# The attention's first key and value loads issued during the last prologue chunks instead of in one block

## The chip, the cores and the metric

The kernel runs on one core of one Trainium2 chip. The metric is the device time of one execution in microseconds; lower is better. The times of before are 1974.73, 1968.76 and 1974.77 us, median 1974.73 us. One further execution was profiled.

## What is computed

One transformer block over `x` (4096 rows of 512) with cross-attention to a context of 3202 rows, followed by a state-space recurrence. Cut to what matters here:

```
q, k, v = heads(norm(x), Wq), heads(norm(ctx), Wk), heads(norm(ctx), Wv)   # 8 heads of 64
attn    = softmax(q @ k.T / 8)
x       = x + (attn @ v) @ W_o.T + b_o
u       = (norm(x) @ W_in.T + b_in) @ Bmat
s       = silu(s @ A.T) + u_t          # a scan over the 4096 rows
out     = x + s @ Cmat + mod
```

The keys and values depend on the context alone, so they are made once, in a prologue, and written to two DRAM buffers; the attention reads them back piece by piece.

## The kernel before

**The prologue** is the loop `for c in range(NCH)` from line 607 on. It walks over 26 chunks of the context, 128 rows each; the last has 2 rows. For chunk c it loads chunk c + 5 (`load_chunk`, on SP's DMA queue), normalises chunk c + 3, forms the value product `pv` (L617), turns chunk c + 2 for the matmuls, copies `pv` to the tile `vs` on ACT (L630) and writes `vs` to the DRAM buffer `vd` (L631, SP's queue). After every fourth chunk, and after the last one, comes a group g of key products: for each of the four head pairs hp one product `pk` (L655), its copy with bias to a tile `ks` on ACT (L663) and the write of `ks` to the DRAM buffer `kd` (L668, SP's queue). Group 5 ends with chunk 23; group 6, the last, holds chunks 24 and 25, so its products are 130 keys wide.

The tiles `ks` come from a pool with three buffers. The fourth `ks` of group 6 therefore goes into the buffer of the first one, and ACT may write it only when the first one's DMA to `kd` has landed.

**The loads.** `load_k` (L366, its DMA is L372) and `load_v` (L375, L380) fetch one pair of chunks of the keys or values of one head pair, 128 KB, into the pool `kp`, which has 13 buffers for each, a whole head pair's worth. Before, at c = 25, ahead of the group of key products, the kernel issues 9 loads of keys and 5 of values for the first unit of the attention (`AHEAD_K - 1` and `AHEAD - 1`). In SP's queue they stand as one block of 14, behind the write of `vx` (L636) and ahead of the four `kd` writes of group 6.

**The attention** starts when the loop is done. Its order is set by a planner, the class `Plan`, whose pieces carry costs and due times; the pieces for the first unit are `sample` (L725, matmuls into `sm`), `scores` (L705, matmuls into `s`), `maximum` and `base` (reductions on DVE), `spread` (L747, PE), `weights` (L782, ACT, makes `p` from `s`), `product` (L839, PE, makes `po`) and the query product `pq_o` (L325). Each step of `scores` first issues the load of keys ten steps ahead and of values six steps ahead. In the built kernel the loads of key pieces 9 to 12 and value pieces 5 to 12 thus follow one by one, in between and behind the last `kd` writes.

The attention's PSUM tiles take the banks of the prologue's pools, which are closed before it starts. In the built order of before, the second `sample` matmul waits for ACT, which is reading the last `pk`.

Every DMA on a queue of this kernel waits, before it is issued, for the DMA eight places ahead of it; SP issues strictly in its order.

Of the kernel before, what the change touches and what calls it, by code (L numbers as in the profile page):

```python
# [23 lines left out]
NCH = 26  # L24
# [29 lines left out]
def keys(c):  # L54


    return CK if c < NCH - 1 else REST


def blocks(c):  # L60

    return 2 if c < NDC - 1 else 1


def key0(c):
    return c * CK
# [117 lines left out]
def xattn_ssm_kernel(  # L184
# [100 lines left out]
    def normalize(xt, n, name, later=False, pool=None):  # L285

        fs = factors(stats(xt, n, name, pool), n, name, pool)
        last = partial(scaled, xt, fs, n, name, pool)
        return last if later else last()
# [17 lines left out]
    def m_tile(shape, name):  # L307

        pool = m_pools.pop(0)
        m_pools.append(pool)  # L310
        return pool.tile(shape, F32, tag="m", name=name)
# [54 lines left out]
    def load_k(i, c):  # L366

        Q, hp, half = units[i]
        if half == 0 or Q == NQB - 1:
            t = kp.tile([P, 2 * CK], F32, tag="k", name=f"k_{Q}_{hp}_{half}_{c}")  # L370
            n = blocks(c) * CK
            nc.sync.dma_start(t[:, :n], kd[hp, c, :, :n])  # L372
            kts[Q, hp, c] = t

    def load_v(i, c):  # L375
        Q, hp, half = units[i]
        if half == 0 or Q == NQB - 1:
            t = kp.tile([CK, 2, P], F32, tag="v", name=f"v_{Q}_{hp}_{half}_{c}")
            n = blocks(c)
            nc.sync.dma_start(t[:, :n], vd[hp, c, :, :n])  # L380
            vts[Q, hp, c] = t
# [5 lines left out]
    steps = [(i, c) for i in range(len(units)) for c in range(NDC)]  # L387
    AHEAD_K, AHEAD, REF = 10, 6, 7
# [12 lines left out]
    def fetch_w(k, queue, part=slice(0, NC)):  # L401
        queue.dma_start(raw[k][:, part], wsrc[:, part, k * H : (k + 1) * H])

    def gain(k, w, i=None):
        for i in range(NC) if i is None else (i,):
            nc.vector.tensor_scalar(
                w[:, i, :], raw[k][:, i, :], g1s[:, i : i + 1], None, ALU.mult
            )

    def weighted(w, by, name):  # L410

        t = wp.tile([P, H], F32, tag="weighted", name=name, bufs=2)
        nc.vector.tensor_scalar(t, w[:, 0, :], by[:, 0:1], None, ALU.mult)
        for i in range(1, NC):
            nc.vector.scalar_tensor_tensor(t, w[:, i, :], by[:, i : i + 1], t, ALU.mult, ALU.add)
        return t

    def shift(k):

        t = weighted(raw[k], be1s, f"shift_{k}")  # L420
        yield
        pb = m_tile([P, 512], f"pb_{k}")
        for o in range(NC):
            nc.tensor.matmul(
                pb[:, o : o + 1], t[:, o * P : (o + 1) * P], ones[:, 0:1],
                start=True, stop=True,
            )
        yield
        nc.vector.tensor_tensor(
            bias[:, k * NC : (k + 1) * NC],  # L430
            pb[:, :NC],
            bqkv[:, k * NC : (k + 1) * NC],
            ALU.add,
        )
        yield
# [104 lines left out]
    def load_chunk(c):  # L540
        if c < NCH:
            n = keys(c)
            xt = cin.tile([CK, H], F32, tag="cx", name=f"cx_{c}", bufs=6)
            nc.sync.dma_start(xt[:n], ctx_in[key0(c) : key0(c) + n, :])
            cxs[c] = xt

    def norm_chunk(c):
        if c < NCH:
            xhs[c] = normalize(cxs.pop(c), keys(c), f"c{c}", pool=cin)
# [27 lines left out]
    with tc.manual_schedule():  # L577
        load_chunk(0)
        nc.scalar.dma_start(g1s, g1)
        fetch_w(2, nc.scalar, slice(0, NC // 2))  # L580
        fetch_w(2, nc.sync, slice(NC // 2, NC))
        load_chunk(1)
        load_chunk(2)
        fetch_w(1, nc.sync)
        load_chunk(3)
        idle = m_tile([P, 512], "idle")
        nc.scalar.copy(bu, neg_half)
        for _ in range(11):
            nc.tensor.matmul(idle[:, :P], a_t, a_t, start=True, stop=True)
        for t, src in ((be1s, beta1), (bqkv, b_qkv), (g2s, g2), (be2s, beta2)):  # L590
            nc.sync.dma_start(t, src)
        for c in range(4, 5):
            load_chunk(c)
        early = [first_chunk(c) for c in range(2)]
        next(early[0])
        next(early[0])
        turn_chunk(0)
        gain(2, wv, 0)
        gain(2, wv, 1)
        next(early[1])  # L600
        gain(2, wv, 2)
        norm_chunk(2)
        gain(2, wv, 3)
        next(early[1])
        work = side()
        first = shift(1)
        for c in range(NCH):
            load_chunk(c + 5)
            norm_chunk(c + 3)
            g, n = c // GC, keys(c)  # L610
            ct, o = cts[g], key0(c) - key0(g * GC)
            pv = kps.tile([P, 512], F32, tag="v", name=f"pv_{c}")
            parts = 1 if c < NCH - 1 else 2
            for i in range(NC // parts):
                for h in range(parts):
                    k = h * NC // parts + i
                    nc.tensor.matmul(  # L617
                        pv[h * HD : h * HD + n, :H],
                        ct[:, k, o : o + n],
                        wv[:, k, :],  # L620
                        start=(i == 0),
                        stop=(i == NC // parts - 1),
                        skip_group_check=True,
                    )
            if c == 0:
                turn_chunk(1)
            turn_chunk(c + 2)
            if c < NCH - 1:
                vs = cin.tile([CK, NC, P], F32, tag="vs", name=f"vs_{c}")
                nc.scalar.copy(vs, pv)  # L630
                nc.sync.dma_start(vd[:, c // 2, :, c % 2, :].rearrange("h p d -> p h d"), vs)  # L631
            else:
                second = wp.tile([n, H], F32, name="second")
                nc.scalar.copy(second, pv[HD : HD + n])
                nc.vector.tensor_tensor(vx[:n], pv[:n], second, ALU.add)
                nc.sync.dma_start(vx[HD : HD + n], vx[:n])  # L636
            if c < GC:
                if c == 1:
                    gain(1, wk)
                for _ in range((0, 0, 1, 2)[c]):  # L640
                    next(first)
            else:
                next(work, None)
            if c % GC < GC - 1 and c < NCH - 1:
                continue
            n_g = o + n
            if c == NCH - 1:
                for k in range(AHEAD_K - 1):
                    load_k(*steps[k])
                for k in range(AHEAD - 1):  # L650
                    load_v(*steps[k])
            for hp in range(NC):
                pk = kps.tile([P, 512], F32, tag="k", name=f"pk_{g}_{hp}")
                for i in range(NC):
                    nc.tensor.matmul(  # L655
                        pk[:, :n_g],
                        wk[:, i, hp * P : (hp + 1) * P],
                        ct[:, i, :n_g],
                        start=(i == 0),
                        stop=(i == NC - 1),  # L660
                    )
                ks = cin.tile([P, GC * CK], F32, tag="ks", name=f"ks_{g}_{hp}")
                nc.scalar.activation(  # L663
                    ks[:, :n_g], pk[:, :n_g], AF.Identity, bias=bias[:, NC + hp : NC + hp + 1]
                )
                for b in range(g * GC, c + 1, 2):
                    m, k = blocks(b // 2) * CK, key0(b) - key0(g * GC)
                    nc.sync.dma_start(kd[hp, b // 2, :, :m], ks[:, k : k + m])  # L668
                if g == 0:
                    nc.gpsimd.tensor_copy(kx[:, hp, REST:], ks[:, : HD - REST])  # L670
                elif c == NCH - 1:
                    nc.gpsimd.tensor_copy(kx[:, hp, :REST], ks[:, CK : CK + REST])
                for _ in range(2 if g > 1 else 1):
                    next(work, None)
        left = sum(1 for _ in work)
        assert left == 0, left
# [1316 lines left out]
```

## Time and profile before

| | |
|---|---|
| runs, us | 1974.73, 1968.76, 1974.77 |
| profiled execution, us | 1970.81 |
| its span in the trace, us | 1969.0 |
| granted TensorE clock, mean | 0.994 |
| PE busy, share of the span | 98% |
| DVE, ACT, POOL busy | 74%, 60%, 12% |

The profiled execution's own time is 1.8 us longer than the span that the trace covers. Times in the rows are microseconds from the start of the span. PE is the matmul engine and PEld its weight loads, DVE, ACT and POOL the other engines; SPq is SP's queue, on which the DMAs in question are issued. In a timeline a row gives the start, the time it takes (rows of the same kind are merged, with their number behind the x), the engine, the line, and in brackets the idle time before it and what ended that. A table of windows gives the busy time of each engine in a stretch, then the granted clock (1.00 is full speed), the share of time for which the DMA engines were busy, and the rate.

### The profile page before, as it was taken

The numbers are of one execution on the slowest core, as the hardware profiler recorded it, in microseconds if no ns is written. First come the engines' busy times: TensorE is split into PE (matmuls) and PEld (weight loads), VectorE is DVE, ScalarE is ACT, GpSimd is POOL, SyncE is SP. The second block draws the span as 40 slices with busy tenths as digits, with TensorE's granted clock in tenths as the row PEclk, the third lists the DMA queues.
The fourth block names the chain that finished last, engine by engine and source line by source line (L and its number), as shares of the span: only waits on it lengthen the run. The fifth ranks groups of instructions, "written<-read, shape, count | busy, mean of one in ns | idle before, by whom it ended". The sixth has DMA issues, their size and how long they took to land. (4 is left out here: it accounts for less than half of the span.)

```text
span 1969.0 us, 66936 instructions
## 1 busy us (share of the span) xinstructions
PE 1932.5 (98%) x29092; PEld 1260.9 (64%) x29092; DVE 1460.6 (74%) x1983; ACT 1172.2 (60%) x1632; POOL 227.3 (12%) x374
## 2 busy tenths in 40 slices
PE   9999899999999999999999999999999999999997
PEld 5444477666666666666667666666666676765674
DVE  4320289688877887788868887888788886877776
ACT  2233377566666666666656665666666675665653
POOL 2121000001200120002100120012001210011105
PEclk9999899999999999999999999999999999999999
DMA  6532323223432243232422342224322331544576
GB/s 195 171 104 62 100 80 99 71 80 89 125 85 83 74 113 82 70 100 78 111 61 88 91 125 79 80 85 115 88 76 78 103 91 45 152 129 133 153 192 218
DMA packets 246934, 204.28 MB, mean 104 GB/s; under 512 B 80808, under 2 KB 220072, under 8 KB 246636
## 3 DMA queue, kind: packets, MB, share of 16 engines
q1 hardware_dynamic: 242616, 193.32, 34.2%
q10 hardware_dynamic: 4020, 6.62, 1.2%
q8 instruction: 231, 3.78, 0.8%
q14 instruction: 67, 0.55, 0.1%
HBM read 156.32 MB, written 29.88 MB: 95 GB/s over the span
## 5 line engine op out<-in xcount | busy, mean ns | idle before, releaser
L782 ACT ACTIVATE p<-s,shifts 128x1024 f32<-128x1024 f32 (+1 forms) x832 | 891.0, 1082 | 482.7 <-PE s L705 474.3
L790 DVE TENSOR_TENSOR acc<-p,acc 128x1024 f32<-128x1024 f32 (+1 forms) x704 | 830.8, 1180 | 205.1 <-ACT p L782 171.3
L705 PE MATMUL s<-q,k 64*64 64x256 f32 x12800 | 836.8, 378 | 1.8 <-ACT p L782 1.8
L839 PE MATMUL po<-p,v 64*64 64x256 f32 x12800 | 835.4, 377 | 3.3 <-DVE o L888 2.9
L705 PEld LDWEIGHTS s<-q,k 64*64 64x64 f32 x12800 | 491.3, 133 | 215.2 <-issue 14.9
L839 PEld LDWEIGHTS po<-p,v 64*64 64x64 f32 x12800 | 485.4, 133 | 194.2 <-issue 13.0
L1109 POOL TENSOR_TENSOR xr<-xr,rowb 128x512 f32<-128x512 f32 x30 | 44.4, 1494 | 987.4 <-DMA xr<-in_x_dram 846.4
L911 DVE RECIPROCAL rd<-rd 128x256 f32<-128x256 f32 (+1 forms) x64 | 110.2, 1722 | 12.9 <-ACT rd L906 12.5
L325 PE MATMUL pq<-xn,wq 128*128 128x512 f32 x248 | 110.7, 598 | 0.0
L1115 PE MATMUL pa<-wo,o 128*128 128x512 f32 x240 | 107.0, 599 | 0.0
L617 PE MATMUL pv<-wv,ct 128*128 128x512 f32 (+1 forms) x208 | 92.6, 595 | 0.8 <-ACT ct L575 0.8
L655 PE MATMUL pk<-ct,wk 128*128 128x512 f32 (+1 forms) x224 | 88.9, 550 | 0.0
L575 DVE COPY ct<-tp_c 128x512 f32<-128x512 f32 (+1 forms) x13 | 8.4, 649 | 105.8 <-PE tp_c L296 105.8
L790 DVE TENSOR_TENSOR acc<-p,p 128x1024 f32<-128x1024 f32 x64 | 78.1, 1220 | 10.5 <-ACT p L782 10.5
L325 PEld LDWEIGHTS pq<-xn,wq 128*128 128x128 f32 x248 | 45.7, 190 | 55.5 <-issue 54.3
L1115 PEld LDWEIGHTS pa<-wo,o 128*128 128x128 f32 x240 | 44.4, 190 | 56.0 <-issue 55.3
L814 DVE TENSOR_TENSOR acc<-swap,acc 64x256 f32<-64x256 f32 x126 | 61.8, 490 | 11.1 <-ACT swap L809 9.4
L663 ACT ACTIVATE ks<-pk,bias 128x512 f32<-128x512 f32 (+1 forms) x28 | 18.0, 642 | 82.6 <-PE pk L655 66.7
L655 PEld LDWEIGHTS pk<-ct,wk 128*128 128x128 f32 x224 | 39.2, 190 | 42.6 <-issue 42.6
L617 PEld LDWEIGHTS pv<-wv,ct 128*128 128x128 f32 (+1 forms) x208 | 36.9, 186 | 43.2 <-issue 41.0
L809 ACT COPY swap<-acc 64x256 f32<-64x256 f32 x126 | 50.8, 404 | 17.4 <-DVE acc L797 14.9
L334 ACT ACTIVATE q<-pq,bias 128x512 f32<-128x512 f32 x31 | 21.3, 688 | 62.5 <-PE pq L325 62.5
(222 smaller groups left out, 1220.1 us busy)
## 6 DMA issues: line engine op xcount, KB each, us to landing
k<-kd SPq DMA_DIRECT2D x432, 128.0 KB, 2.3
v<-vd SPq DMA_DIRECT2D x432, 128.0 KB, 2.2
xn<-x SPq DMA_DIRECT2D x416, 32.0 KB, 1.9
xr<-in_x_dram SPq DMA_DIRECT2D x30, 256.0 KB, 3.7
x1d<-xr SPq DMA_DIRECT2D x30, 256.0 KB, 2.2
x<-in_x_dram SPq DMA_DIRECT2D x28, 256.0 KB, 3.3
cx<-in_ctx_dram SPq DMA_DIRECT2D x25, 256.0 KB, 3.9
vd<-vs SPq DMA_DIRECT2D x25, 256.0 KB, 2.4
```

The source lines that it names most:

```text
L325: nc.tensor.matmul(pq, wq[:, i, hp * P : (hp + 1) * P], xn[:, i, :], start=(i == 0), stop=(i == NC - 1),)
L617: nc.tensor.matmul(pv[h * HD : h * HD + n, :H], ct[:, k, o : o + n], wv[:, k, :], start=(i == 0), stop=(i == NC // parts - 1), skip_group_ ...
L655: nc.tensor.matmul(pk[:, :n_g], wk[:, i, hp * P : (hp + 1) * P], ct[:, i, :n_g], start=(i == 0), stop=(i == NC - 1),)
L705: nc.tensor.matmul(s[k0 : k0 + HD, a, b, :], kts[(*w["at"][:2], c)][r, b * CK + k0 : b * CK + k0 + HD], q[r], start=True, stop=True, skip_ ...
L782: nc.scalar.activation(t[:, :, :nb, :], w["ps"][c][:, :, :nb, :], AF.Exp, bias=w["shift"])
L790: nc.vector.tensor_tensor(w["acc"][:, :, :nb, :], t[:, :, :nb, :], before[:, :, :nb, :], ALU.add)
L809: nc.scalar.copy(w["swap"][r], of[(1 - k) * HD : (2 - k) * HD])
L814: nc.vector.tensor_tensor(of[r], w["swap"][r], of[r], ALU.add)
L839: nc.tensor.matmul(w["po"][a * HD : (a + 1) * HD, k, :QU], vts[Q, hp, c][r, b, a * HD : (a + 1) * HD], t[r, a, b, :], start=(c == 0 and b ...
L911: nc.vector.reciprocal(w["rd"][:, part], (w["pd"] if last else w["rd"])[:, part])
L1109: nc.gpsimd.tensor_tensor(v["x"], v["x"], rowb, ALU.add)
L1115: nc.tensor.matmul(v["pa"], o_t[Q, c, half][:, t * P : (t + 1) * P], wo[:, c, :], start=(c == 0), stop=(c == NC - 1),)
```

## The change

The block of 14 loads ahead of the last group of key products goes. Instead the loop takes them from a list, up to four in a chunk, from chunk 20 on, right after `load_chunk`:

```diff
         first = shift(1)
+        loads = [partial(load_k, *steps[k]) for k in range(AHEAD_K - 1)]
+        loads += [partial(load_v, *steps[k]) for k in range(AHEAD - 1)]
         for c in range(NCH):
             load_chunk(c + 5)
+            if c >= 2 * AHEAD_K:
+                for _ in range(4):
+                    if loads:
+                        loads.pop(0)()
             norm_chunk(c + 3)
...
             n_g = o + n
-            if c == NCH - 1:
-                for k in range(AHEAD_K - 1):
-                    load_k(*steps[k])
-                for k in range(AHEAD - 1):
-                    load_v(*steps[k])
             for hp in range(NC):
```

With 14 loads and four in a chunk, chunks 20 to 23 take 4, 4, 4 and 2. No load is added or left out. The instructions of PE, DVE, ACT and POOL keep their order; SP's DMAs alone change theirs. The order that is built puts some of the planner's own loads further ahead too. From chunk 20 on SP's queue is now (k0 is the load of key piece 0, v0 of value piece 0; `kd` 5.1 is the write of group 5, head pair 1):

```
before  cx 25 | vd 20 | vd 21 | vd 22 | vd 23 | kd 5.0 x2 | kd 5.1 x2 | kd 5.2 x2 | kd 5.3 x2
        vd 24 | vx | k0 to k8 | v0 to v4 | kd 6.0 | kd 6.1 | kd 6.2 | k9 | v5 | k10 | kd 6.3
        v6 | k11 | v7 | k12 | v8 to v12
after   cx 25 | k0 to k3 | vd 20 | k4 to k7 | vd 21 | k8 v0 v1 v2 k9 | vd 22 | v3 v4 v5 | vd 23
        kd 5.0 x2 | k10 v6 k11 | kd 5.1 x2 | v7 | kd 5.2 x2 | kd 5.3 x2 | vd 24 | vx
        kd 6.0 | kd 6.1 | kd 6.2 | k12 | kd 6.3 | v8 to v12
```

After, k10 waits for the first write of `kd` 5.0, k11 for the second and k12 for that of `kd` 6.0, since they read what these write.

## The prediction

> **What bounds the kernel now.** I read the page's shares first (PE is busy for 98% of the span), then windows of 20 us for a place where PE is not full, then the waits of that place, then the timelines of the queue and engines that the waits name. The stretch around the change, and everything behind it:
>
> ```profile
> 160.00:180.00 20.00, 20.00 (x57) 9.39 (x56) 1.36 (x3) 6.91 (x11) 0.00 (x0) 1.00 0.18 58
> 180.00:200.00 20.00, 20.00 (x54) 9.08 (x53) 0.26 (x2) 4.34 (x7) 1.03 (x3) 1.00 0.16 48
> 200.00:220.00 20.00, 16.53 (x67) 8.40 (x65) 0.68 (x1) 4.34 (x8) 0.56 (x3) 0.96 0.36 111
> 220.00:240.00 20.00, 15.27 (x190) 9.24 (x194) 8.16 (x13) 9.11 (x11) 0.19 (x1) 0.78 0.41 121
> ...
> 240.00:1940.00 1700.00, 1685.80 (x27976) 1133.98 (x27968) 1373.84 (x1777) 1089.29 (x1489) 177.85 (x253) 1.00 0.35 98
> ```
>
> Behind the bounds of a window stand its length and PE's busy time: 20.00 of 20 in the two up to 200 us, then 16.53 and 15.27, with the granted clock (the number after POOL's) down to 0.78. From 240 to 1940 us PE is busy for 1685.80 of 1700 us at full clock. So the kernel is bound by PE, and what PE gets back near 220 us moves all the rest forward. Who PE waits for there (waits between 200 and 240 us: total, times, longest):
>
> ```profile
> ACT ks L663 <- DMA kd<-ks: 8.8, 1, 8.8
> ...
> PE sm L725 <- ACT ks L663: 8.2, 1, 8.2
> ```
>
> One wait of 8.2 us. PE's sample matmul waits for ACT's `ks` of the fourth head pair, and that waits for a write to `kd`, the one whose buffer it reuses. SP's queue, ACT and PE over this time:
>
> ```profile
> 210.41 0.59 ACT L630 COPY vs<-pv 128x512 f32<-128x512 f32 x1 [2.70 <-PE pv L617]
> 211.02 0.37 SPq L631 DMA_DIRECT2D vd<-vs  x1
> 213.36 0.37 ACT L663 ACTIVATE ks<-pk,bias 128x130 f32<-128x130 f32 x1 [0.55 <-PE pk L655]
> 213.59 0.74 SPq L636 DMA_DIRECT2D vx<-vx  x1
> 214.38 4.18 SPq L372 DMA_DIRECT2D k<-kd  x9
> 215.89 0.64 PE L725 MATMUL sm<-q,kx 64*64 64x256 f32 x2
> 218.60 2.33 SPq L380 DMA_DIRECT2D v<-vd  x5
> 221.04 1.34 SPq L668 DMA_DIRECT2D kd<-ks  x3
> 224.31 0.37 ACT L663 ACTIVATE ks<-pk,bias 128x130 f32<-128x130 f32 x1 [8.78 <-DMA kd<-ks]
> 224.73 0.70 PE L725 MATMUL sm<-q,kx 64*64 64x256 f32 x3 [8.20 <-ACT ks L663]
> 225.23 3.58 PE L705 MATMUL s<-q,k 64*64 64x256 f32 x28
> 225.89 0.76 DVE L739 TENSOR_REDUCE m<-sm 128x1 f32<-128x256 f32 x2 [12.37 <-PE sm L725]
> 226.68 0.16 DVE L740 TENSOR_TENSOR m<-m 128x1 f32<-128x1 f32 x1
> 229.07 3.70 PE L325 MATMUL pq_o<-xn,wq 128*128 128x512 f32 x8
> 230.56 2.12 ACT L782 ACTIVATE p<-s,shifts 128x1024 f32<-128x1024 f32 x2
> ```
>
> The first `ks` of group 6 is ready at 213.36 + 0.37 = 213.73. SP is then busy with `vx` until 214.33 and with the 14 loads from 214.38 to 220.93, and starts that `ks`'s write at 221.04 only. PE ends its first sample matmuls at 215.89 + 0.64 = 216.53 and stands until 224.73. What the pause does to the clock:
>
> ```profile
> 218.00:218.50 0.50, 0.00 (x0) 0.00 (x0) 0.00 (x0) 0.00 (x0) 0.00 (x0) 0.91 0.90 283
> 218.50:219.00 0.50, 0.00 (x0) 0.00 (x0) 0.00 (x0) 0.00 (x0) 0.00 (x0) 0.50 0.78 221
> ...
> 228.00:228.50 0.50, 0.50 (x9) 0.26 (x7) 0.00 (x0) 0.00 (x0) 0.00 (x0) 0.50 0.56 162
> 228.50:229.00 0.50, 0.50 (x14) 0.30 (x6) 0.00 (x0) 0.00 (x0) 0.00 (x0) 0.85 0.75 194
> ...
> 224.73:228.62 3.89, 3.89 (x37) 2.28 (x40) 0.91 (x3) 0.00 (x0) 0.19 (x1) 0.50 0.62 178
> ```
>
> A mean of 0.91 over 218.00 to 218.50 is full clock until about 218.4 and half after it: the drop comes 1.9 us after PE went idle. The clock is whole again near 228.6, so PE's first 3.89 us after the pause run at half speed.
>
> **What is removed.** The 14 issues, (220.93 - 214.38) / 14 = 0.47 us each, no longer stand between `vx` and the write of `ks` 6.0. That write takes the place of the first load, at 214.38. How long it takes to land is known from its kind:
>
> ```profile
> DMA to landing us min/median/max: 1.7/1.7/1.8
> ...
> DMA to landing us min/median/max: 2.9/2.9/2.9
> ...
> DMA to landing us min/median/max: 1.7/1.8/3.7
> ...
> DMA to landing us min/median/max: 1.8/6.0/6.2
> ```
>
> These are the `kd` writes between 195 and 216 us, the very write of 221.04 behind 14 loads in flight, those between 100 and 125 us, and those between 35 and 45 us. 221.04 + 2.9 = 223.94, and ACT starts at 224.31: 0.37 from landing to ACT. Then 0.37 for ACT itself and 0.05 to PE. With 1.7, as the queue ahead of it holds only `vd` 24 (issued at 211.02) and `vx`: 214.38 + 1.7 + 0.37 + 0.37 + 0.05 = 216.87 for PE's restart. It saves 224.73 - 216.87 = **7.86 us** and leaves a pause of 0.34 us. The bounds: no pause at all gives 8.20; the slow landing of 2.9 gives 218.07, thus 6.66 with a pause of 1.54 us.
>
> **What goes with it.** Both pauses are shorter than the 1.9 us after which the clock fell, so I take the clock to stay. The 3.89 us at 0.50 then take half: **1.95 us** saved. That holds if PE, not DVE, sets the pace there: DVE began 225.89 - 224.73 = 1.16 us after the restart, at full clock half of that, 0.6, and L739 and L740 take 0.95 (to 226.84), thus 1.55 us after the restart. The score matmuls start 0.25 after it and take 3.58 / 2 = 1.8, until 2.05. The spread matmuls behind them find the maximum ready.
>
> The Trainium skill, "TensorE: Matmul & The Clock Gate", Part 1: The HAM clock gate, lets the clock fall after an idle window of about 3.4 us, in windows that run on their own. Here it fell after 1.9 us of idle, so the measurement decides, and the sum is the same by either, as 0.34 us is under both; the two part in the first rival.
>
> **What is added.** Nothing; 14 loads move ahead, and with them k9, k10, k11, v5, v6 and v7, which the built order pulls into chunks 22 to 23 and group 5. At 0.47 us each, at most five stand together (k8, v0, v1, v2, k9): 2.3 us of SP. SP has that time:
>
> ```profile
> SPq L631 <- ACT vs L630: 25.0, 5, 7.8
> SPq L668 <- ACT ks L663: 14.3, 5, 3.6
> ...
> 169.01 0.33 SPq L544 DMA_DIRECT2D cx<-in_ctx_dram  x1
> 172.33 21.39 SPq L631 DMA_DIRECT2D vd<-vs  x4
> 197.39 11.14 SPq L668 DMA_DIRECT2D kd<-ks  x8
> ...
> 192.75 0.59 ACT L630 COPY vs<-pv 128x512 f32<-128x512 f32 x1 [5.25 <-issue]
> 200.11 0.69 ACT L663 ACTIVATE ks<-pk,bias 128x512 f32<-128x512 f32 x1 [2.75 <-PE pk L655]
> ```
>
> Between 165 and 213 us it waits 25.0 us for `vs` copies and 14.3 us for `ks`, up to 7.8 us at a time. The first four loads fit behind the last `cx` load (169.34 to 171.2) ahead of `vd` 20 at 172.33. Without that cover a `vd` write would be 2.3 us late; its buffer is wanted again three chunks on (the copy of 192.75 reuses the one written at 172.33), so nobody would wait. PE, ACT and DVE have no instruction behind SP there. The transfers find the DMA engines at 0.18 and 0.16, in the first windows above; I cost all this at nothing.
>
> New are waits on SP: k10 and k11 for the writes of `kd` 5.0, with `kd` 5.1 behind them. With a landing of 1.7 us k10 is issued at 197.39 + 1.7 = 199.1, then v6 and k11 until about 200.5; the second `ks` of the group is done at 200.11 + 0.69 = 200.8. It hides. k12 waits for `kd` 6.0 (landed at 216.1), ahead of `kd` 6.3, whose `ks` is done at 216.82. `kd` 6.3 is issued near 216.9 and lands before 219.8 even with 2.9 us; the first `p`, which takes that room in SBUF, is due at 230.56 - 9.8 = 220.8. v8 to v12 keep their distance to `kd` 6.3.
>
> **Sum.** 7.86 + 1.95 = 9.8 us; the bounds give 6.66 + 1.95 = 8.6 and 8.20 + 1.95 = 10.15. Against the profiled execution's own 1970.81 us (span 1969.0 and 1.8 around it): 1961.0. The median of the runs, 1974.73, is 3.9 above it and one run 2.1 below; among these four executions the middle is (1970.81 + 1974.73) / 2 = 1972.8. From there the forecast is **1963.0 us**. Its own range is 1968.76 - 10.15 = 1958.6 to 1974.77 - 8.6 = 1966.2. A measurement here tells no change from one of about 0.3%, 5.9 us.
>
> **Rivals.** *The write lands late and the clock falls once more.* With 3.7 us, the longest `kd` landing once the weights are in (above), PE restarts at 218.87 after 2.34 us, past the 1.9 us: 5.86 us are won and nothing from the clock, 1972.8 - 5.9 = 1966.9, on the border of 0.3%. For it: 3.7 occurred. Against: at 214.38 no load is in flight. By the page's window of 3.4 us the clock would hold and the gain be 7.8.
>
> *The wait isn't removed*, because something other than the loads holds it: 1972.8. The write's start 0.11 us after the last load speaks against it. If a landing of 6.2 us recurred, the restart would be at 221.37 and the gain 3.4 us, 1969.4, also within 0.3%.
>
> *Slower: SP is blocked by its own reads.* If `kd` writes land after L us, k10 holds SP until 197.39 + L, `kd` 5.1's second half is issued 1.8 us later and lands at 199.2 + 2L; the first `ks` of group 6, which takes its buffer at 213.36, delays PE from L = 6.9 us on. The gain is used up at L = 11.8, and 0.3% is lost at L = 14.8 (9.8 + 5.9 = 15.7 us more in 2L): 1978.7 us. The longest L seen is 6.2, among the first weights; around 200 us it is 1.8.
>
> **How the numbers follow.** Forecast 80%, late landing with the clock 10%, wait not removed or half of it 6%, slower 4%. Faster by over 0.3%: nearly all of the first and half of the second, 0.83; within it 0.13; slower 0.04. The forecast's range, opened to 1957.5 for a lower run and to 1968.5 for most of the first rival, is the range.
>
> **What would show it.** In the profile of the changed kernel: `kd` 6.0 issued right behind `vx` near 214.4; PE's wait before the sample matmuls under 1.6 us, where it was 8.2; granted clock 1.00 throughout 200 to 240 us; the first `p` near 220.8; no wait of ACT or PE between 170 and 213 us that was not there before; the stretch behind unchanged but earlier. I am wrong if PE's busy time drops in the windows from 160 to 200 us, if the pause stays over 1.9 us, or if a wait of `p` or `po` for a DMA takes up what was won.

## The result

The changed kernel takes 1960.49 us (median of 6 runs, 1959.07 to 1964.69), the kernel before in the same series 1972.45 us (6 runs, 1968.76 to 1974.77). The ratio is 0.9944, 95% interval 0.9929 to 0.996: 11.0 us faster (7.9 to 14.0). The profiled executions are 1970.81 and 1960.71 us, 10.1 us apart.

The windows around the start of the attention, in the profile after (columns as before: length, busy time of PE, PEld, DVE, ACT and POOL, granted clock, DMA share, GB/s):

```profile
160.00:180.00 20.00, 20.00 (x57) 9.38 (x56) 1.45 (x3) 6.86 (x11) 0.00 (x0) 1.00 0.37 112
180.00:200.00 20.00, 20.00 (x54) 9.13 (x53) 0.17 (x1) 4.33 (x7) 1.02 (x3) 1.00 0.34 99
200.00:220.00 20.00, 19.74 (x114) 10.57 (x114) 2.11 (x7) 4.83 (x10) 0.74 (x4) 1.00 0.38 120
220.00:240.00 20.00, 20.00 (x327) 13.24 (x329) 14.21 (x13) 15.03 (x16) 0.00 (x0) 1.00 0.03 9
```

PE now lacks 0.26 us of the 40 from 200 to 240, where it lacked 8.20 before, and the clock is 1.00 in all of them. The loads show as DMA share 0.37 and 0.34 where it was 0.18 and 0.16; PE stays at 20.00 of 20 there. PE's wait for `ks` (waits of 200 to 240 us: total, times, longest):

```profile
PE sm L726 <- ACT ks L664: 0.3, 1, 0.3
```

And the timeline of SP's queue, ACT and PE over the last key products:

```profile
212.02 3.84 PE L656 MATMUL pk<-ct,wk 128*128 128x130 f32 x32
213.27 0.37 ACT L664 ACTIVATE ks<-pk,bias 128x130 f32<-128x130 f32 x1 [0.55 <-PE pk L656]
213.49 0.74 SPq L642 DMA_DIRECT2D vx<-vx  x1
214.35 1.57 SPq L669 DMA_DIRECT2D kd<-ks  x3
216.04 0.35 SPq L372 DMA_DIRECT2D k<-kd  x1
216.27 0.37 ACT L664 ACTIVATE ks<-pk,bias 128x130 f32<-128x130 f32 x1 [0.84 <-PE pk L656]
216.66 0.32 SPq L669 DMA_DIRECT2D kd<-ks  x1
216.69 0.44 PE L726 MATMUL sm<-q,kx 64*64 64x256 f32 x3 [0.26 <-ACT ks L664]
219.12 3.70 PE L325 MATMUL pq_o<-xn,wq 128*128 128x512 f32 x8
220.60 2.12 ACT L783 ACTIVATE p<-s,shifts 128x1024 f32<-128x1024 f32 x2
224.53 1.04 PE L840 MATMUL po<-p,v 64*64 64x256 f32 x16
```

The write of `ks` 6.0 follows `vx` at 214.35 instead of 221.04; ACT's fourth `ks` starts at 216.27 instead of 224.31, PE's sample matmuls at 216.69 instead of 224.73, the first `p` at 220.60 instead of 230.56.

For all comparisons below I take one distance within each trace, from the start of the last group's first `pk` to the start of the first `po`: it holds the whole disputed place, and what varies elsewhere between executions drops out. In the profile before its two ends are

```profile
212.12 3.84 PE L655 MATMUL pk<-ct,wk 128*128 128x130 f32 x32
...
234.48 1.04 PE L839 MATMUL po<-p,v 64*64 64x256 f32 x16
```

that is 22.36 us before and 224.53 - 212.02 = 12.51 us after: **9.85 us**. The 10.1 us between the profiled executions are this place almost alone.

### The profile page after: what moved, and what is told of

Its sections match the earlier page's. It is cut to its first block, busy times and chain, and to the rows that moved or that the text cites. A ratio compares the mean times of both kernels' runs of the same rounds, so it can differ in the third digit from the quotient of the medians.

```text
span 1958.9 us, 66935 instructions
## 1 busy us (share of the span) xinstructions
PE 1928.9 (98%) x29092; PEld 1259.3 (64%) x29092; DVE 1459.3 (74%) x1983; ACT 1171.3 (60%) x1632; POOL 225.5 (12%) x374
```

## The experiments

Two theories stood against mine, which was that the time came from the place of the write `kd` 6.0 in SP's queue and from the clock: that the early landing of the keys and values is what helps, and that the transfers in flight held the write. Each kernel of this table was timed beside the kernel before. The distances are worked out as above from the start of `pk` and of the first `po` in each trace. Each gain in the last column lies inside what the interval of its ratio allows.

| kernel | us, median | kernel before | ratio, 95% interval | `pk` to `po`, us | gain in it |
|---|---|---|---|---|---|
| changed | 1960.49 | 1972.45 | 0.9944 (0.9929 to 0.996) | 12.51 | 9.85 |
| block behind the products | 1968.08 | 1974.1 | 0.9961 (0.9947 to 0.9975) | 16.35 | 6.01 |
| own buffer for the fourth `ks` | 1968.66 | 1974.1 | 0.9968 (0.9958 to 0.9979) | 18.04 | 4.32 |
| filler on PE | 1970.86 | 1974.1 | 0.9985 (0.9975 to 0.9996) | 20.59 | 1.77 |
| `kd` writes from ACT's queue | 1962.92 | 1974.1 | 0.9944 (0.993 to 0.9957) | 12.39 | 9.97 |
| 4 loads left | 1964.15 | 1972.5 | 0.9957 (0.9943 to 0.9971) | 14.69 | 7.67 |
| 8 loads left | 1968.46 | 1972.5 | 0.9981 (0.9971 to 0.9991) | 18.71 | 3.65 |
| all 14 in chunk 20 | 1962.55 | 1972.5 | 0.9948 (0.9933 to 0.9962) | 12.51 | 9.85 |

**The block behind the last key products.** The kernel before with

```diff
-            if c == NCH - 1:
-                for k in range(AHEAD_K - 1): load_k(*steps[k])
-                for k in range(AHEAD - 1): load_v(*steps[k])
             for hp in range(NC):
...
+        for k in range(AHEAD_K - 1): load_k(*steps[k])
+        for k in range(AHEAD - 1): load_v(*steps[k])
         left = sum(1 for _ in work)
```

> The block of 14 loads is issued behind the last key products, so that SP's queue has vx, kd 6.0 to 6.3, then k0 to k8, v0 to v4. My theory (the time came from the place of kd 6.0 in SP's queue): kd 6.0 is issued near 214.4 and ACT's fourth ks starts near 216.4 as in the changed kernel, but k0 is now issued only near 217.0 and lands near 219.2 (2.2 us), so PE stands some 2.3 us before the first score matmul, and the first p comes near 223 if the clock holds, 224 to 225 if it falls: 5.5 to 7.5 us faster than before, 2.5 to 4.5 us slower than the changed kernel. Rival (the gain came from the early landing of the keys and values, the place of kd 6.0 does not matter): no gain, 1972 us.

Its timeline:

```profile
216.23 0.37 ACT L658 ACTIVATE ks<-pk,bias 128x130 f32<-128x130 f32 x1 [0.83 <-PE pk L650]
217.00 4.35 SPq L372 DMA_DIRECT2D k<-kd  x9
219.29 2.44 PE L704 MATMUL s<-q,k 64*64 64x256 f32 x32 [1.98 <-DMA k<-kd]
223.35 2.12 ACT L781 ACTIVATE p<-s,shifts 128x1024 f32<-128x1024 f32 x2
```

ACT's `ks` comes as early as in the changed kernel, though no load has moved ahead: the place of `kd` 6.0 alone does that. Then PE stands 1.98 us for k0, and the clock falls afterwards (at 220.6, for 3.4 us). It is 6.0 us faster than before, inside 5.5 to 7.5, and the rival that knows only the early landing falls. The rest of the changed kernel's gain is lost here because the loads now come later than before: k0 is issued at 217.00 instead of 214.38, and 12.51 becomes 16.35. Whether landing earlier than before is worth anything, this kernel can't say; the writes from ACT's queue below can.

**A buffer of its own for the fourth `ks`.** The block stays where it was:

```diff
-                ks = cin.tile([P, GC * CK], F32, tag="ks", name=f"ks_{g}_{hp}")
+                if c == NCH - 1 and hp == NC - 1:
+                    ks = cin.tile([P, CK + REST], F32, tag="ksl", name="ks_last", bufs=1)
+                else:
+                    ks = cin.tile([P, GC * CK], F32, tag="ks", name=f"ks_{g}_{hp}")
```

> The kernel before, but the fourth ks of the last group has a buffer of its own and waits for no write to kd. The block of loads stays ahead of the kd writes. My theory: PE's wait of 8.2 us before the sample matmuls goes wholly, the query product ends near 222.7, but the kd writes are still issued from 221.0 to 222.9 and land near 225.5, and the first p, which takes room that they read from, waits for them: the first p near 225 to 226 instead of 230.6 (before) and 220.6 (changed kernel), PE pauses some 2 to 4 us behind the query product, 4.5 to 5.5 us faster than before. Rival (the reuse of the ks buffer is the whole story): first p near 220.6, 10 us faster, as the changed kernel.

```profile
219.02 3.70 PE L325 MATMUL pq_o<-xn,wq 128*128 128x512 f32 x8
222.49 1.28 SPq L671 DMA_DIRECT2D kd<-ks  x3
223.89 0.35 SPq L671 DMA_DIRECT2D kd<-ks_last  x1
225.86 2.12 ACT L785 ACTIVATE p<-s,shifts 128x1024 f32<-128x1024 f32 x2 [5.23 <-DMA kd<-ks_last]
227.03 3.54 PE L708 MATMUL s<-q,k 64*64 64x256 f32 x32 [4.31 <-ACT p L785]
```

The wait of the prediction is gone, and the next one in line takes its place: the first `p`, in room that the `kd` writes read from, waits for the last of them, and PE stands 4.31 us behind the query product. So the buffer is the first thing that is held up, but not the cause; the cause is that the four writes stand behind the block. The first `p` came as expected; the gain of 4.32 us is a little under the 4.5 to 5.5. The writes began at 222.49 instead of 221.0, 0.9 us of it a wait of SP for an earlier load of `k` to land, and PE's pause was longer than the 2 to 4 us expected. The clock then fell at 227.24, so that `po` starts 3.30 us after the score matmuls of 227.03, where the changed kernel takes 1.78.

**PE kept busy.** The kernel before with work for PE in its pause, whose result nobody uses:

```diff
+        fill = m_tile([P, 512], "fill")
+        for _ in range(9):
+            nc.tensor.matmul(fill, wk[:, 0, :P], wk[:, 1, :], start=True, stop=True)
         left = sum(1 for _ in work)
```

> The kernel before, with nine 128x512 matmuls behind the last key products, whose result nobody uses; they fill 7.7 us of PE's pause. My theory (the half-speed stretch after the pause is due to PE's standing still): granted clock 1.00 throughout, restart of the sample matmuls still at 224.7, the query product begins 1.95 us earlier than the 229.07 of before, 1.9 us faster than before (1970.5 against 1972.45). Rival (the stretch is slow because the loads are in flight, or because a new kind of matmul begins): no gain, clock 0.50 after 224.7 or score matmuls as slow as before.

```profile
216.08 7.89 PE L677 MATMUL fill<-wk 128*128 128x512 f32 x18
225.16 0.44 PE L728 MATMUL sm<-q,kx 64*64 64x256 f32 x3 [0.61 <-ACT ks L663]
227.58 3.70 PE L325 MATMUL pq_o<-xn,wq 128*128 128x512 f32 x8
...
224.00:228.00 4.00, 3.38 (x49) 2.16 (x50) 1.22 (x5) 0.37 (x1) 0.18 (x1) 1.00 0.69 190
```

The restart is as late as before (12.76 us behind the start of `pk`, 12.61 before), but from it to the query product PE takes 227.58 - 225.16 = 2.42 us, as in the changed kernel (219.12 - 216.69 = 2.43), where the kernel before took 229.07 - 224.73 = 4.34. The clock is 1.00 with the loads in flight as before (DMA share 0.69). The half-speed stretch is thus the pause's, and its price here is 1.91 us.

**The `kd` writes of the last group from ACT's queue**, while SP issues the block:

```diff
-                    nc.sync.dma_start(kd[hp, b // 2, :, :m], ks[:, k : k + m])
+                    queue = nc.scalar if c == NCH - 1 else nc.sync
+                    queue.dma_start(kd[hp, b // 2, :, :m], ks[:, k : k + m])
```

> The kernel before, with the four kd writes of the last group issued from ACT's queue, right behind the ks that they write, while SP issues its block of 14 loads. My theory (place in SP's queue): kd 6.0 is issued near 213.9 and lands within 1.7 to 2.9 us, PE restarts between 216.6 and 217.6, clock 1.00: 8.8 to 10 us faster than before, within 1 us of the changed kernel. Rival (the transfers in flight delay the write, whoever issues it): kd 6.0 lands only when the block has, near 221 to 223, less than 3 us faster.

```profile
213.60 0.35 ACTq L669 DMA_DIRECT2D kd<-ks  x1
214.21 4.45 SPq L372 DMA_DIRECT2D k<-kd  x9
216.09 0.37 ACT L663 ACTIVATE ks<-pk,bias 128x130 f32<-128x130 f32 x1 [0.78 <-PE pk L655]
220.42 2.12 ACT L783 ACTIVATE p<-s,shifts 128x1024 f32<-128x1024 f32 x2
```

PE has no wait at all there, and the gain is the changed kernel's (9.97 against 9.85; the ratios are equal), with the block where it always was. `kd` 6.0 is ahead of the first load by 0.6 us in this kernel, so it doesn't show what a write in the midst of the block costs; the fourth write does, issued at 216.5: it took 3.4 us to land, and nobody waited for it. The block stands at its old time here and the gain is whole. So landing the loads earlier than before is worth nothing here; what costs is landing them later, as with the block behind.

**Some loads left behind.** The changed kernel, with n = 4 or 8 loads still between `vx` and the writes:

```diff
                 for _ in range(4):
-                    if loads:
+                    if len(loads) > n:
                         loads.pop(0)()
...
+            if c == NCH - 1:
+                for load in loads:
+                    load()
             for hp in range(NC):
```

> The changed kernel, but the last 4 of the 14 loads (v1 to v4) stay between vx and the kd writes; only 10 move ahead. My theory: kd 6.0 is issued 4 x 0.47 = 1.9 us later, near 216.3, lands after 1.7 to 2.5 us, and PE pauses 2.2 to 3.0 us. If the clock falls after about 1.9 us of pause, as in the kernel before, the score matmuls run at half speed for a while and the kernel is 3.5 to 5 us slower than the changed one; if it needs a whole idle window of 3.4 us, 1.9 to 2.7 us slower.

> The changed kernel, but 8 of the 14 loads (k6 to k8, v0 to v4) stay between vx and the kd writes. My theory: kd 6.0 is issued 8 x 0.47 = 3.8 us later, near 218.2, PE pauses 4.1 to 5.3 us, the clock falls: 5.7 to 7 us slower than the changed kernel, 3 to 4 us faster than before. The pause grows by 0.47 us with each load left. Rival (the wait goes with the block as a whole, for example with the transfers in flight): the pause does not grow with the number.

With 4 loads left, and below with 8:

```profile
216.42 1.32 SPq L672 DMA_DIRECT2D kd<-ks  x3
219.11 0.44 PE L729 MATMUL sm<-q,kx 64*64 64x256 f32 x3 [2.45 <-ACT ks L667]
...
218.00:219.00 1.00, 0.00 (x0) 0.00 (x0) 0.00 (x0) 0.32 (x1) 0.00 (x0) 1.00 0.44 100
219.00:220.00 1.00, 0.89 (x16) 0.67 (x20) 0.20 (x1) 0.05 (x1) 0.18 (x1) 1.00 0.89 261
```

```profile
217.94 1.39 SPq L672 DMA_DIRECT2D kd<-ks  x3
221.09 0.69 PE L729 MATMUL sm<-q,kx 64*64 64x256 f32 x3 [4.80 <-ACT ks L667]
...
221.00:222.00 1.00, 0.92 (x9) 0.56 (x13) 0.00 (x0) 0.03 (x1) 0.18 (x1) 0.54 0.78 232
224.00:225.00 1.00, 1.00 (x19) 0.57 (x14) 0.00 (x0) 0.00 (x0) 0.00 (x0) 0.75 0.71 203
```

The pause is 0.26, 2.45, 4.80 and 8.20 us for 0, 4, 8 and 14 loads: it grows by 0.57 us with each, more than the 0.47 us of its issue. The rest is landing: `kd` 6.0 took 1.5, 1.9, 2.3 and 2.9 us from its issue in these four traces, 0.1 us for each load ahead of it (in further executions 2.1 and 1.9 with 4 loads, 3.0 and 2.7 with 14). If that is the transfers' doing, which no run shows apart from the number of loads, their rival is right in a small part, 1.4 of the 7.94 us that ACT's fourth `ks` came sooner. With 8 the clock falls, and the distance is 6.20 us longer than the changed kernel's, inside 5.7 to 7. With 4, after 2.45 us of standing, the clock stayed at 1.00, and the distance is 2.18 us longer, as expected for that case.

**The clock once more.** That last row went against the reading of 1.9 us in the prediction, so the same kernel was profiled twice more, and the kernel before as well.

> The kernel of e4_leave_4 once more, for its clock. In e4_leave_4 PE paused 2.45 us and the clock stayed at 1.00, while in the kernel before it fell 1.9 us after the pause began. Theory: the clock is decided at the ends of windows of 3.4 us that run on their own (half-speed stretches so far: 10.3, 3.4, 3.4 and 3.4 us), and falls if more than about half of a window was idle; a pause of 2.45 us then falls into one window or is cut by an end, by chance, and in about 7 of 10 executions the clock falls for 3.4 us and costs up to 1.7 us. Rival: a pause of 2.45 us is too short for the clock; it stays at 1.00 again.

> As e7_leave_4_b, a third execution: by the theory of windows the pause of about 2.45 us makes the clock fall in some executions and not in others, always for a multiple of 3.4 us; by the rival it stays at 1.00 each time.

> The kernel before in another execution, for its clock. By the theory of windows of 3.4 us the pause of 8.2 us always makes the clock fall, but how long the matmuls run at half speed after it depends on where the next window ends: between 3.4 us and some 6 us, which costs 1.7 to 3 us; the first profile had 3.9 us (1.95). The wait of 8.2 us itself stays, within 0.3 us. Rival: the half-speed stretch is 3.9 us each time.

> As e8_before_b, a third execution: by the theory of windows a stretch between 3.4 and some 6 us that differs from the other two, by the rival 3.9 us again.

The kernel with 4 loads left, second and third execution:

```profile
219.30 0.69 PE L729 MATMUL sm<-q,kx 64*64 64x256 f32 x3 [2.71 <-ACT ks L667]
...
218.00:219.00 1.00, 0.00 (x0) 0.00 (x0) 0.00 (x0) 0.13 (x1) 0.00 (x0) 0.67 0.60 130
225.00:226.00 1.00, 1.00 (x4) 0.52 (x3) 0.00 (x0) 1.00 (x3) 0.00 (x0) 0.92 0.27 76
```

```profile
219.05 0.48 PE L729 MATMUL sm<-q,kx 64*64 64x256 f32 x3 [2.52 <-ACT ks L667]
...
219.00:220.00 1.00, 0.95 (x12) 0.73 (x16) 0.01 (x1) 0.00 (x0) 0.18 (x1) 0.66 0.97 263
222.00:223.00 1.00, 1.00 (x19) 0.61 (x14) 0.00 (x0) 0.00 (x0) 0.00 (x0) 0.64 0.67 189
```

and the third execution of the kernel before:

```profile
224.90 0.70 PE L725 MATMUL sm<-q,kx 64*64 64x256 f32 x3 [8.01 <-ACT ks L663]
...
220.00:221.00 1.00, 0.00 (x0) 0.00 (x0) 0.00 (x0) 0.00 (x0) 0.00 (x0) 0.76 0.92 289
230.00:231.00 1.00, 1.00 (x2) 0.35 (x2) 0.20 (x2) 0.67 (x2) 0.00 (x0) 0.62 0.52 139
```

Pauses of the same length (2.45, 2.71, 2.52 us) left the clock whole once and brought it down twice, in the last only after PE had restarted. A mean of 0.67 over 218 to 219 places the fall at 218.34, one of 0.92 over 225 to 226 the rise at 225.16: 6.8 us; in the third 219.32 and 222.72: 3.4 us. The second execution of the kernel before was like the first (22.38 us from `pk` to `po`); in the third the fall came at 220.52 and the rise at 230.76, so that 5.86 us behind the restart ran at half speed and the distance was 23.09 us. From the restart to the end of the query product these two took 4.26 + 3.70 and 4.67 + 4.27 us, the changed kernel 2.43 + 3.70: the clock's share in the kernel before is thus 1.8 to 2.8 us by execution, not a fixed 1.95. Both rivals fall, that a pause of 2.45 us always leaves the clock whole and that the half-speed stretch is 3.9 us each time; what the theory says is weighed at the end.

**All 14 loads in chunk 20**: the changed kernel with `for _ in range(14)` in place of `range(4)`.

> The changed kernel, but all 14 loads are issued in chunk 20 at once. My theory: SP has the time there (it waits for vs copies), vd 20 is issued near 175.9 instead of 172.2 and nobody waits for it; first p near 220.6 and the same time as the changed kernel, within 0.5 us in the trace. Rival (the spreading itself matters, a block of 14 delays what is behind it wherever it stands): a wait of PE or ACT of 1 us or more between 172 and 200 us, slower than the changed kernel by that.

```profile
212.07 3.84 PE L656 MATMUL pk<-ct,wk 128*128 128x130 f32 x32
...
224.58 1.04 PE L840 MATMUL po<-p,v 64*64 64x256 f32 x16
```

The distance is 12.51 us, the changed kernel's to the hundredth. `vd` 20 goes out at 175.96, there is no wait of PE between 100 and 240 us but the 0.3 us for `ks`, and ACT's waits between 170 and 213 us are the changed kernel's. That the loads are spread over chunks adds nothing; what counts is that they leave the place ahead of the `kd` writes.

## Why the prediction was right

**What bounds.** Right: PE's one long pause, 8.20 us, is now 0.26, and the windows behind are as full as before, only earlier.

**The write's new place.** `kd` 6.0 was put at 214.38 and came at 214.35. I took 1.7 us for its landing, as for the larger writes before it; it took 1.5. The row of 216.27 puts ACT's wait down to `pk`, but in the kernel with a buffer of its own, where the copy waits for no write, it starts 3.88 us after the start of `pk` and here 4.25: the landing still ends this wait, and the 0.26 us of PE are what is left of it. The restart, forecast at 216.87, was at 216.69; 0.10 of that is a prologue that ran so much earlier in this execution (212.02 against 212.12). The term of 7.86 us measured 224.31 - 212.12 less 216.27 - 212.02, 7.94: 6.59 from the issue and 1.4 from the landing. The prediction had both in one term and put 1.2 us of it (2.9 - 1.7) down to the landing; the series of loads left parts them.

**The clock.** The term of 1.95 us measured 4.34 - 2.43 = 1.91, and the filler shows it by itself. Sum 9.85 against the forecast 9.81.

**What was costed at nothing** was nothing: PE is full in the windows from 160 to 200 us, and ACT's waits between 170 and 213 us are those of before within 0.1 us. Of the reads that now wait on SP for their own writes, k10 was forecast at 199.1 and the second pair of writes to be on time (`ks` 5.1 done at 200.70):

```profile
199.05 0.32 SPq L372 DMA_DIRECT2D k<-kd  x1
199.94 0.38 SPq L372 DMA_DIRECT2D k<-kd  x1
200.73 0.79 SPq L669 DMA_DIRECT2D kd<-ks  x2
```

k11 is done at 200.32 and the pair goes out at 200.73: a slack of 0.4 us on SP, so this cover is thin. Behind it `kd` 6.3 was issued at 216.66 (forecast 216.9), in time for `p`; the own-buffer kernel shows what that wait costs when it isn't.

**Where a step was wrong.** "Both pauses are shorter than the 1.9 us after which the clock fell" took one distance in one execution for a limit. The conclusion held, 0.26 us being far from it; the first rival did not. It had the clock fall at a pause of 2.34 us, and the runs show that at 2.5 us it falls or not by the execution, sometimes only after PE has restarted; in one execution 1.76 us of standing had been enough when it fell. Nor did the write land late: 1.5 us.

**The time.** Forecast 1963.0, measured 1960.49, by the ratio 11.0 us (7.9 to 14.0) where the sum was 9.8. The interval holds the sum. One of the three profiles of the kernel before took 0.7 us longer over the disputed place than the other two, because of the clock; whether that is where the median's further microsecond comes from was not shown.

## What to carry to other kernels

Look at what stands ahead of a store in its queue as closely as at the store: here 14 loads held a write of 64 KB for 6.6 us, and the buffer that it read from was due. Two orders that took the store from behind the loads, earlier loads and another queue, won the same; moving the loads behind the store won less, since they then came later than they were needed. Freeing the buffer alone moved the wait to the next user of the memory. When such a wait goes, count the clock with it: in these traces a pause after which the clock fell cost 1.5 to 2.8 us more behind its end.

## What the runs showed of the hardware

Wherever the clock fell at the pause, its fall and its rise lie a multiple of 3.4 us apart: 10.24 (before, in each of the three executions), 3.4 (block behind), 3.4 (own buffer), 3.4 (8 loads left), 6.8 and 3.4 us (4 left, second and third). This is what the Trainium skill, "TensorE: Matmul & The Clock Gate", Part 1, says of windows of 3413 ns that run on their own, and here the trace agrees. What brings it down is less than a whole idle window, though. Taking the 3.41 us that end at each fall as such a window, and PE's pause from the timelines:

| execution | pause | fall | idle in the window that ends there | idle in the one before, which kept the clock |
|---|---|---|---|---|
| before | 216.53 to 224.73 | 218.4 | 1.87 us, 55% | none |
| before, second | 216.54 to 224.84 | 218.37 | 1.83 us, 54% | none |
| before, third | 216.88 to 224.90 | 220.52 | 3.4 us, all | 0.2 us |
| 4 left, second | 216.58 to 219.30 | 218.34 | 1.76 us, 52% | none |
| 4 left, third | 216.53 to 219.05 | 219.32 | 2.52 us, 74% | none |
| block behind | 217.31 to 219.29 | 220.64 | 1.98 us, 58% | 0.3 us |
| 8 left | 216.28 to 221.09 | 221.08 | 3.4 us, all | 1.39 us, 41% |
| own buffer | 222.72 to 227.03 | 227.24 | 3.2 us, 94% | 1.11 us, 33% |

All of them fit a limit between 41% and 52% of a window, an estimate from these rows. The pause of 2.45 us that left the clock whole fits too, if a window's end cut it near its middle, which its trace can't show. Nothing but these executions was tried, and where a window ends is read off the fall itself, so the limit is a reading, not a rule.
